# Graph attention on one core: the order of deep blocks in a batch's last two tiles, and who weighs them

## The chip, the core and the metric

The kernel runs on one core of a Trainium2 chip. The time is the device time of one launch in microseconds; lower is better. A core has five engines that run their own instruction queues in order and meet through semaphores: PE (TensorE, matmuls; PEld is its weight load), DVE (VectorE), ACT (ScalarE), POOL (GpSimd, which also issues the indirect DMAs) and SP (SyncE, which issues plain DMAs). The time before is the median of three runs, 1906.49 us (1903.19 to 1907.76).

## The reference

The layer is graph attention with a residual and a normalisation, for 16 batches of 1024 nodes with 512 features, 8 heads of 64. The adjacency matrix is the same for all batches and very sparse: a few nodes have many neighbours, most have a handful.

```python
def _L0_gnn_ref(x, adj, Wq, bq, Wk, bk, Wv, bv, Wo, bo):
    q = (x @ Wq + bq).reshape(b, n, H, HD)
    k = (x @ Wk + bk).reshape(b, n, H, HD)
    v = (x @ Wv + bv).reshape(b, n, H, HD)
    scores = jnp.einsum('bqhd,bkhd->bhqk', q, k) / jnp.sqrt(jnp.float32(HD))
    scores = scores + (1.0 - adj)[None, None, :, :] * -1000000000.0
    attn = jax.nn.softmax(scores, axis=-1)
    out = jnp.einsum('bhqk,bkhd->bqhd', attn, v).reshape(b, n, d)
    return out @ Wo + bo
x = _layernorm(x + _L0_gnn_ref(...), axis=-1)
```

## The kernel before

**Sparse work in tiles and blocks.** The nodes are ranked by their number of neighbours, and each batch is cut into 8 tiles of 128 nodes in that order. For each query the kernel gathers only the key and value rows that it has an edge to. The unit of this is a *block*: 128 gathered rows of keys and values (`kvg`, 128 x 1024 f32, 512 KB). In an *own* block `i` of a tile, row p holds the i-th neighbour of the tile's query p; `OWN` says how many own blocks each tile has. Nodes with more neighbours than that put the rest into *deep* blocks, in which 128 left-over edges of any queries of the tile stand side by side; `BLOCKS` says how many.

```python
OWN = (2, 1, 2, 3, 4, 5, 5, 7)
BLOCKS = (0, 0, 0, 0, 0, 0, 1, 5)
```

So tile 6 has 5 own blocks and 1 deep one, tile 7 has 7 and 5. Tile 1 (one key) takes no blocks: its value row `V1` is gathered alone and transposed with `turn` when block (7, 4) of its batch is reached. Tile 0 is worked on in batches 0 and 1 and in every odd batch, there for two batches at once. In all there are 530 blocks: 34 in batches 0, 1 and the odd ones, 32 in the even ones from 2 on. Of them 105 are first own blocks (i = 0), 329 further own blocks, and 96 deep ones.

**What a block costs.** `gather` issues the indirect DMA of the block's key and value rows on POOL (L1230), and for a deep block one of its query rows `qg` too (L1184), for an own block with i = 0 a plain load of the tile's query rows `qt` on SP (L1217). `products` multiplies query and key rows on DVE (L1251), `scores` sums them for each head on DVE (L1255), `exponentials` takes the exponential on ACT (L1266). `weigh` multiplies the value rows with the eight heads' weights: on ACT as eight activations of 128x64 (L1276), or on DVE as one instruction of 128x512 (L1280); `by_act` decides. An own block's weighed rows are then added to the tile's first ones on DVE (`add_own`, L1292). A deep block's rows are added by PE instead, which multiplies them with a 0/1 matrix `sums` that says to which query each row belongs (`add_up`, L1301 and L1302, four matmul instructions in all), into one PSUM buffer with the tag "sum". `normalise` divides a tile's rows by their sums on DVE when the next tile's first block comes, and for tiles 6 and 7 adds the PSUM buffer to the own sum first (L1313, L1314).

**The order.** All of it is written out by hand: a step n of the main loop (from L1470 on) emits the exponentials of block n+3, the products of n+4, the gathers up to n+8, the weighing of n+1 if DVE does it, the adding of n, the scores of n+4, the weighing of n+2 if ACT does it, and the deep sum of n. Each engine runs its own instructions in this order. The list `blocks` sets what block n is; before, a tile's own blocks come first and its deep blocks after them:

```python
blocks = [(b, t, i) for b in range(B) for t in tiles_of(b) if t != ONE_KEY for i in range(OWN[t] + BLOCKS[t])]
```

Between these steps PE works on the *fronts* of batches to come (transposes of x and the products for queries, keys and values, `pq`, `x`, `pp`, `z`) and on the output products `po` of tiles that are done. How many of these units a step gets is a credit: a share for the batch, weighted by `paced` with `load_of`, which counts the DVE work of a step. The results leave PSUM on DVE (q, w, g, kv) and on ACT, a step later. `KG_BUFS` = 8 buffers hold the gathered rows; a buffer is free again when its block has been weighed. Five buffers with the tag "qt" hold `qg` and `V1`.

**Who weighs.** `by_act` gives ACT all own blocks with i > 0; of all other blocks (first own and deep) it gives ACT those with an even n, and the first 17 of the program, except in the last batch, where DVE weighs them. In batches 1 to 14 this gives ACT 5 of 7 first blocks in odd batches and 4 of 6 in even ones, and 2 of 6 deep blocks in both.

Of the kernel before, what the change touches and what calls it, by code (L numbers as in the profile page):

```python
# [26 lines left out]
OWN = (2, 1, 2, 3, 4, 5, 5, 7)  # L27
BLOCKS = (0, 0, 0, 0, 0, 0, 1, 5)
# [6 lines left out]
LONE, ONE_KEY, ONE_KEY_AT, ONE_KEY_LAST = 64, 1, (7, 4), (3, 0)  # L35
# [142 lines left out]
def kernel(  # L178
# [37 lines left out]
    B, N, D = x.shape  # L216
# [13 lines left out]
    own = [SHORT_KEYS * t for t in SHORT]  # L230
# [3 lines left out]
    NBT = NB - OWN[ONE_KEY]  # L234
# [19 lines left out]
    with ExitStack() as main:  # L254
# [82 lines left out]
        def merged(b):  # L337
            return b >= PAIRED_FROM and b % 2 == 1

        def tiles_of(b):  # L340
            return [t for t in range(NT) if t or b < PAIRED_FROM or merged(b)]
# [828 lines left out]


        KG, QG, PV, PSUM, QT, RDEN, V1 = {}, {}, {}, {}, {}, {}, {}
        blocks = [(b, t, i) for b in range(B) for t in tiles_of(b) if t != ONE_KEY for i in range(OWN[t] + BLOCKS[t])]
        start = [min(n for n, block in enumerate(blocks) if block[0] == b) for b in range(B)] + [len(blocks)]

        def load_more():
# [90 lines left out]

        def by_act(n):
            b, t, i = blocks[n]
            return 0 < i < OWN[t] or n < total - NBT and (n % 2 == 0 or n < NBT // 2)  # L1270

        def weigh(n):
            v, pv = KG.pop(n), PV[n]
            if by_act(n):
                for h in range(HEADS):
                    nc.scalar.activation(  # L1276
                        pv[:, ts(h, HD)], v[:, ds(D + h * HD, HD)], AF.Copy, scale=pv[:, D + h:D + h + 1]
                    )
                return
            nc.vector.tensor_tensor(  # L1280
                pv[:, 0:D].rearrange("p (h d) -> p h d", d=HD),
                v[:, D:].rearrange("p (h d) -> p h d", d=HD),
                pv[:, D:, None].to_broadcast([P, HEADS, HD]), op=OP.mult,
            )
# [134 lines left out]
        total = len(blocks)  # L1419
# [4 lines left out]
        def load_of(n):  # L1424

            b, t, i = blocks[n]
            had = 2.0 + (not by_act(min(n + 1, total - 1))) + (0 < i < OWN[t])
            if i == 0:
                had += 3.0 if BLOCKS[blocks[n - 1][1]] else 1.3
            return had  # L1430
# [17 lines left out]
        with tc.manual_schedule():  # L1448
# [20 lines left out]
            n = -LEAD_IN  # L1469
            while n < total or plan or rest or urgent or done or finishing or spilled or lone_tiles or not guarded:  # L1470
# [6 lines left out]
                elif n in start:  # L1477

                    b = start.index(n)
                    left = sum(u[0] for u in fronts)  # L1480
# [11 lines left out]
                if 0 <= n + 1 < total and not by_act(n + 1):  # L1492
                    weigh(n + 1)
# [96 lines left out]
```

## Time and profile before

| | |
|---|---|
| median of the runs | 1906.49 us |
| the profiled execution | 1892.33 us, of which the span of the trace is 1890.4 us |
| mean granted PE clock | 0.989 |
| HBM traffic | 298 GB/s over the span |
| DVE scores, L1255 | 530 x 680 ns |
| DVE adding of own blocks, L1292 | 329 x 693 ns |
| gathers of key and value rows on POOL | 530, median 1017 ns each in the kv_pair ones, 6.4 us from issue to landing |

The profile shows one execution. An engine's busy time counts the time in which at least one of its instructions ran; the mean of one instruction is larger than busy time divided by number, because instructions overlap at their ends. Eight activations of one weighing on ACT take 8 x 864.6/3432 = 2.015 us. "Idle before" is the time for which an engine stood still ahead of an instruction, with what ended it. The prologue, in which the adjacency matrix is read and ranked, ends at about 136 us; after it a batch takes 100 to 134 us, and the last 26 us finish the output.

### The profile page before, as it was taken

How to read it: one execution, taken by the hardware profiler on the slowest of the kernel's cores; microseconds unless marked ns; L12 is line 12 of the kernel's file. 1: busy time of each engine (PE TensorE's matmuls, PEld its weight loads, DVE VectorE, ACT ScalarE, POOL GpSimd, SP SyncE). 2: the span in 40 equal slices, each digit the busy share in tenths (PEclk: the TensorE clock that was granted, in tenths of full speed). 3: DMA queues.
4: the chain of work that ended last, by engine and by line, in shares of the span. 5: the costliest groups of instructions: out<-in, count | busy, mean ns of one | idle time of the engine just before them, and what ended most of it. 6: DMA issues, size and time to landing. Idle time of an engine off the chain costs nothing. (4 is left out here: it accounts for less than half of the span.)

```text
span 1890.4 us, 25101 instructions
## 1 busy us (share of the span) xinstructions
PE 1815.1 (96%) x5149; PEld 878.2 (46%) x5149; DVE 1700.6 (90%) x3484; ACT 1531.7 (81%) x6016; POOL 1267.4 (67%) x1189
## 2 busy tenths in 40 slices
PE   7989999999999999999999999999999999999995
PEld 3434444444545454444445444444445444444442
DVE  6888889999999999899899989899999999997874
ACT  3627869979888988979798978989898989886794
POOL 1367766777677676757677676767666777656774
PEclk9989999999999999999999999999999999999997
DMA  7357787988889898888889898999889899989993
GB/s 280 114 168 226 233 307 227 315 295 294 308 287 316 305 328 283 305 288 307 312 292 335 271 334 274 314 304 310 301 307 326 293 356 310 314 277 340 334 319 117
DMA packets 188149, 544.63 MB, mean 288 GB/s; under 512 B 32602, under 2 KB 32622, under 8 KB 187986
## 3 DMA queue, kind: packets, MB, share of 16 engines
q0 software_dynamic: 116400, 382.82, 60.6%
q1 hardware_dynamic: 68510, 154.30, 21.8%
q10 hardware_dynamic: 3076, 5.82, 0.9%
q14 instruction: 120, 0.98, 0.2%
q8 instruction: 43, 0.70, 0.1%
HBM read 419.52 MB, written 144.34 MB: 298 GB/s over the span
## 5 line engine op out<-in xcount | busy, mean ns | idle before, releaser
L1276 ACT ACTIVATE pv<-kvg,pv 128x64 f32<-128x64 f32 x3432 | 864.6, 340 | 0.0
L1230 POOL DMA_INDIRECT kvg<-kv_pair,place_row x462 | 526.7, 1140 | 258.0 <-ACT pv L1276 73.3
L790 PE MATMUL po<-wo,oT 128*128 128x512 f32 x816 | 380.1, 596 | 1.0 <-ACT oT L1340 0.9
L790 PE MATMUL pq<-wq,xT 128*128 128x512 f32 x792 | 368.9, 597 | 0.4 <-DVE g L966 0.4
L1255 DVE TENSOR_REDUCE s<-qk 128x8 f32<-128x512 f32 x530 | 360.2, 680 | 7.5
L1251 DVE TENSOR_TENSOR qk<-qt,kvg 128x512 f32<-128x512 f32 x434 | 296.4, 683 | 22.2 <-DMA kvg<-kv_pair,place_row 22.1
L947 PE MATMUL pp<-t,s 128*128 128x512 f32 x504 | 237.4, 593 | 2.7 <-ACT sq_k L800 1.7
L947 PE MATMUL x<-b,xT 128*128 128x512 f32 x504 | 237.8, 594 | 0.8 <-ACT e L960 0.8
L790 PEld LDWEIGHTS po<-wo,oT 128*128 128x128 f32 x816 | 152.6, 191 | 166.8 <-issue 153.9
L1292 DVE TENSOR_TENSOR pv<-pv,pv 128x520 f32<-128x520 f32 x329 | 228.0, 693 | 0.7 <-ACT pv L1276 0.6
L790 PEld LDWEIGHTS pq<-wq,xT 128*128 128x128 f32 x792 | 149.2, 192 | 166.4 <-issue 155.0
L1266 ACT ACTIVATE pv<-s,absent 128x8 f32<-128x8 f32 x434 | 126.3, 293 | 79.8 <-DVE s L1255 76.2
L1001 POOL DMA_INDIRECT x<-in_x_dram,asked_row x120 | 130.2, 1085 | 88.3 <-PE pxT L748 40.5
L1125 POOL DMA_INDIRECT out_dram<-y,asked_row x129 | 144.8, 1122 | 35.7 <-issue 19.8
L800 ACT ACTIVATE sq_k<-kv 128x128 bf16<-128x128 f32 x512 | 150.9, 301 | 6.0 <-DVE kv L970 6.0
L947 PEld LDWEIGHTS pp<-t,s 128*128 128x128 f32 x504 | 94.2, 190 | 114.1 <-issue 101.4
L947 PEld LDWEIGHTS x<-b,xT 128*128 128x128 f32 x504 | 94.3, 191 | 111.5 <-issue 106.5
L1184 POOL DMA_INDIRECT qg<-q_rows,query_row x96 | 106.9, 1114 | 36.5 <-issue 24.7
L947 PE MATMUL z<-b,s 128*128 128x512 f32 x252 | 119.1, 595 | 6.5 <-DVE kv L975 6.5
L1029 POOL DMA_INDIRECT y<-in_x_dram,asked_row x93 | 104.5, 1124 | 27.5 <-issue 25.8
L947 PE MATMUL z<-t,s 128*128 128x512 f32 x252 | 120.0, 599 | 0.0
L947 PE MATMUL pp<-t,xT 128*128 128x512 f32 x252 | 118.4, 592 | 0.0
(276 smaller groups left out, 2766.7 us busy)
## 6 DMA issues: line engine op xcount, KB each, us to landing
kv_pair<-kv SPq DMA_DIRECT2D x98, 512.0 KB
q_rows<-q SPq DMA_DIRECT2D x106, 256.0 KB
qt<-q_rows SPq DMA_DIRECT2D x98, 256.0 KB
residual<-x SPq DMA_DIRECT2D x36, 256.0 KB
y<-residual SPq DMA_DIRECT2D x36, 256.0 KB
kv_rows<-kv SPq DMA_DIRECT2D x15, 512.0 KB
kvg<-kv_pair,place_row POOLq DMA_INDIRECT x462, 6.5
kv_pair<-kv SPq DMA_DIRECT2D x28, 256.0 KB
```

The lines of the kernel that those rows point to most:

```text
L790: nc.tensor.matmul(p, lhs(c), w[:, c, :], start=(c == 0), stop=(c == NPAIR - 1))
L800: nc.scalar.activation(sq, s[:, ts(h, P)], AF.Square, scale=scale, accum_out=sums[:, h:h + 1])
L947: nc.tensor.matmul(R[bank], l[:, ts(c, P)], right[:, c, :], start=(first and c == 0), stop=(c == 1), skip_group_check=True,)
L1001: nc.gpsimd.indirect_dma_start(out=y, out_offset=None, in_=x_rows, in_offset=bass.IndirectOffsetOnAxis(ap=asked_row[:, t:t + 1], axis=0), ...
L1125: nc.gpsimd.indirect_dma_start(out=out_rows[b, t], out_offset=bass.IndirectOffsetOnAxis(ap=rows, axis=0), in_=y, in_offset=None, element_o ...
L1184: nc.gpsimd.indirect_dma_start(out=q, out_offset=None, in_=q_rows[b % ROWS], in_offset=bass.IndirectOffsetOnAxis(ap=rows, axis=0))
L1230: nc.gpsimd.indirect_dma_start(out=KG[n], out_offset=None, in_=rows, in_offset=bass.IndirectOffsetOnAxis(ap=(place_row if b else key_row)[ ...
L1251: nc.vector.tensor_tensor(QK[n], q, KG[n][:, 0:D], op=OP.mult)
L1255: nc.vector.tensor_reduce(S[n], QK.pop(n).rearrange("p (h d) -> p h d", d=HD), axis=AX.X, op=OP.add)
L1266: nc.scalar.activation(PV[n][:, D:], S.pop(n), AF.Exp, bias=bias)
L1276: nc.scalar.activation(pv[:, ts(h, HD)], v[:, ds(D + h * HD, HD)], AF.Copy, scale=pv[:, D + h:D + h + 1])
L1292: nc.vector.tensor_tensor(PV[b, t], PV[b, t], pv, op=OP.add)
```

## The change

Two things change. The new function `blocks_of` gives the order of a tile's blocks: as before in batch 0 and in tiles without deep blocks, and otherwise with the deep blocks spread among the own ones. For tile 6 the order becomes 0, 1, 2, 5, 3, 4 (5 is the deep one), for tile 7 it becomes 0, 1, 7, 2, 8, 3, 9, 4, 10, 5, 11, 6 (7 to 11 are deep). And `by_act` no longer goes by the parity of n: ACT weighs own blocks with i > 0 and never a first block; of the deep blocks it weighs the ones of the program's first 17 blocks (there are none), those with an even n in batch 0, those with b + i even in batches 1 to 14, and none in the last batch.

```diff
-        blocks = [(b, t, i) for b in range(B) for t in tiles_of(b) if t != ONE_KEY for i in range(OWN[t] + BLOCKS[t])]
+
+        def blocks_of(b, t):
+
+            own, deep = list(range(OWN[t])), list(range(OWN[t], OWN[t] + BLOCKS[t]))
+            if b == 0 or not deep:
+                return own + deep
+            spread = max(1, len(own) // (len(deep) + 1))
+            left = len(own) - spread * len(deep)
+            for j, i in enumerate(deep):
+                own.insert(left + j * (spread + 1), i)
+            return own
+
+        blocks = [(b, t, i) for b in range(B) for t in tiles_of(b) if t != ONE_KEY for i in blocks_of(b, t)]
...
         def by_act(n):
             b, t, i = blocks[n]
-            return 0 < i < OWN[t] or n < total - NBT and (n % 2 == 0 or n < NBT // 2)
+            if i < OWN[t]:
+                return i > 0
+            return n < NBT // 2 or (n % 2 == 0 if b == 0 else b < B - 1 and (b + i) % 2 == 0)
```

## The prediction

> **What bounds the kernel now.** I read the totals first, then the chain that ended last, then a table of windows, one for each batch, then who waited for whom, and last the timeline of one batch boundary.
>
> ```profile
> PE 1815.1 (96%) x5149; PEld 878.2 (46%) x5149; DVE 1700.6 (90%) x3484; ACT 1531.7 (81%) x6016; POOL 1267.4 (67%) x1189
> ```
> TensorE (PE) is busy 96%, VectorE (DVE) 90%, ScalarE (ACT) 81%. Busy PE time can hide stretched matmuls, so the chain gives the pace:
>
> ```profile
> 1308.26 3.43 PE pq L790 x8
> ```
> 3.43 us / 8 = 0.429 us for a 512-column matmul instruction, wherever the chain runs through PE; most of the program's matmuls start at that distance. So PE is near its floor. What is left to win is what PE loses in stalls. The windows of nine batches (5 to 13), with the columns window, length, PE, PEld, DVE, ACT, POOL, clock, DMA share, GB/s:
>
> ```profile
> 697.00:806.00 109.00, 105.08 (x305) 51.15 (x303) 99.74 (x195) 92.22 (x376) 75.89 (x69) 1.00 0.87 303
> ...
> 909.00:1011.00 102.00, 100.80 (x294) 49.32 (x295) 99.08 (x196) 92.05 (x378) 74.00 (x68) 1.00 0.89 307
> ...
> sum 934.00, PE 906.93 PEld 442.47 DVE 878.63 ACT 810.96 POOL 649.81; mean PE 100.77 PEld 49.16 DVE 97.63 ACT 90.11 POOL 72.20
> ```
> A batch takes 934.00/9 = 103.78 us; PE is idle 3.0 us of it, DVE 6.15 us. Two engines are nearly full; ACT has 13.7 us left. Who waits, from 270 to 1740 us (batches 1 to 14), in us, times, longest:
>
> ```profile
> DVE qk L1251 <- DMA kvg<-kv_pair,place_row: 25.6, 13, 4.9
> DVE kv L975 <- PE z L947: 11.4, 11, 1.9
> ...
> PE sum L1301 <- DVE pv L1280: 11.0, 4, 3.7
> PE z L947 <- DVE kv L975: 6.1, 5, 2.4
> PE pm L858 <- DVE vsum L854: 5.6, 4, 1.9
> ...
> ACT pv L1266 <- DVE s L1255: 73.1, 66, 6.3
> ```
> PE's largest wait is for a deep block's weighed row, four times, 11.0 us. ACT waits for DVE, not DVE for ACT: making ACT shorter is worth nothing by itself. The largest of the four, at the end of batch 5:
>
> ```profile
> 788.74 1.17 POOL L1184 DMA_INDIRECT qg<-q_rows,query_row  x1 [0.30 <-issue]
> ...
> 796.55 1.01 POOL L1230 DMA_INDIRECT kvg<-kv_pair,place_row  x1 [0.30 <-ACT pv L1276]
> ...
> 804.94 0.69 DVE L1251 TENSOR_TENSOR qk<-qt,kvg 128x512 f32<-128x512 f32 x1 [4.28 <-DMA kvg<-kv_pair,place_row]
> ...
> 806.29 1.22 PE L1301 MATMUL sum<-pv,sums 128*128 128x256 f32 x2 [3.75 <-DVE pv L1280]
> ```
> DVE sat 4.28 us for the gathered rows of batch 6's first block. Their gather was issued at 796.55, 8.4 us before; from 771 us GpSimd (POOL) had no gap longer than the 0.30 us between two issues, because five deep blocks in a row asked for ten gathers (776.00 to 791.2), with stores and x loads behind them. PE then waited 3.75 us, and its clock fell:
>
> ```profile
> 798.65:810.00 11.35, 7.60 (x20) 4.22 (x19) 6.96 (x12) 4.17 (x18) 7.28 (x8) 0.85 1.00 385
> ```
> DMA was full (1.00) there, DVE busy 61%, the clock 0.85. "TensorE: Matmul & The Clock Gate" in the Trainium skill (HAM oscillation) says that PE idle for more than about 3.4 us is throttled; the 0.85 after 3.75 us agrees, and nothing in the sum uses the page.
>
> **The change, part by part.** (1) *Order.* From batch 1 on, tile 6 runs as own 0,1,2, deep, own 3,4 and tile 7 as own 0,1, then deep and own by turns. No instruction is added or removed: 96 deep blocks keep their products, scores, two gathers and two pairs of matmuls. The ten gathers of tile 7's deep blocks were issued in 15.2 us (776.00 to 791.2); they now come one pair for every two steps. At about 3.2 us a step (tile 7 took 762.5 to 799.4, twelve steps, 3.1 us each) that is 10 x 1.3 us of POOL in some 30 us, and the next batch's first gathers no longer stand behind a queue. SP's queue sees none of it: a tile's query rows are loaded with its own block 0, which stays first. What goes: PE's 11.0 us for deep rows, and the clock's loss after them, estimated from the window above as 0.15 x 7.60 = 1.1 us for the one long stall, some 2 us for all four. Bounds: nothing, if other transfers keep the gathers late (DMA share is 0.87 and 0.89 in the batch windows, so there is not much room); at best all the waits of PE listed above, 11.0 + 6.1 + 5.6 = 22.7, with the clock about 25. I take 13 for this: the mechanism is plain in the trace, and POOL's queue is the only thing at that place which the order makes.
>
> "Perfetto Trace Analysis" in the Trainium skill (Optimization Strategy) says that a kernel whose most contended engine changes over time may gain from interleaving these stretches. The trace has the stretches: 745 to 768 us is bound by ACT (22.37 of 23.00 us), 798.65 to 810 by DMA.
>
> (2) *Who weighs.* Before, ACT weighs 429 blocks (3432/8) and DVE 101. After the new rule ACT keeps all 329 own blocks with i > 0 and weighs 44 deep ones: 373; DVE 157. The 56 that move: seven first blocks in batch 0; in each of the seven odd batches 1 to 13 five first blocks go to DVE and two deep ones to ACT, +3, 21 in all; in each of the seven even batches 2 to 14 four first blocks, 28. The last batch changes nothing but its order.
>
> ```profile
> L1276 ACT ACTIVATE pv<-kvg,pv 128x64 f32<-128x64 f32 x3432 | 864.6, 340 | 0.0
> ...
> L1280 DVE TENSOR_TENSOR pv<-kvg,pv 128x512 f32<-128x512 f32 x101 | 68.9, 683 | 0.0
> ```
> ACT loses 56 x 864.6/429 = 56 x 2.015 = 113 us; DVE gains 56 x 0.683 = 38.2 us, of which 7 x 0.683 = 4.8 in batch 0, where 250 to 270 us shows DVE at 16.38 of 20.00 and PE at 20.00: hidden. The other 49 cost 33.5 us, 2.4 us a batch. Their cover is DVE's idle 6.15 us a batch. A batch's floor by DVE becomes 97.63 + 2.4 = 100.0 us, by PE it stays 100.8. So the cover holds on the mean, but it is thin: in the quietest window (909 to 1011) DVE idles 2.92 us, and an odd batch adds 2.05. What is late if it gives way: DVE runs its queue in order, so behind the extra weighing stand the sum of the own blocks, the next scores, then w, g and kv, for which PE waits. Bounds: 0 (all covered) to +33.5 (none). I take +4: about 0.3 us a batch, nearer to the covered end, since DVE's waits (25.6 for gathers, 11.4 for z) are what the order shortens.
>
> A rule against it: "SBUF — State Buffer" (Who interferes with whom) says that a DVE instruction with two SBUF inputs blocks a GpSimd instruction that reads SBUF. If every one of the 49 held up a gather for its length, POOL would be 33.5 us later in all. The trace has gathers of 1017 ns at the median beside a full DVE and 1000 ns in batch 0, where DVE had room, so I give it nothing.
>
> (3) *ACT's relief.* The 113 us are worth nothing where ACT waits for DVE. Where ACT is full (745 to 768 us) it frees the gather buffers late; POOL's gathers waited 88.0 us for ACT's weighing over the whole span. In even batches tiles 6 and 7 now give ACT 12 of 18 blocks, in odd ones 14 as before, without the run of twelve. PE's waits for kv and vsum in these tiles (6.1 + 5.6) might shrink by a third: I take -4, bounds 0 and -11.7 (the same waits as in the upper bound of (1), so not to be added to it).
>
> (4) *Pacing.* `load_of` counts a step's DVE work, so PE's units are dealt out anew within each batch; their number is the same. Of the deep sums, tile 7's first now comes at the tile's third block instead of its eighth, into the one "sum" buffer that tile 6's result has left two steps earlier: two steps are 6 us against 1.5 us for reading it, nothing.
>
> Sum: -13 + 4 - 4 = **-13 us** on the profiled execution, 1890.4 to 1877 us of span (1892.3 to 1879 with the 1.9 around it). That execution lies 14.2 us under the median of the runs, 1906.49; the difference is carried over: **1893.5 us**, -0.7%.
>
> **Rivals.** *DVE takes the bound* (slower). One mechanism: 2.4 us more of DVE work in each of batches 1 to 14, in an engine that idles 6.15 us, while the idle time that it has is waiting that returns in another place. It decides once DVE's busy share of a batch passes about 98%; the quiet batches stand at 97.1% (99.08/102.00) and would come to 99%. All of it on the path, with the 13 us won, is 33.5 - 13 = +20, 1927; half of it +4; with the stalls staying as well and half of it, +17. Centre 1917. For it: ACT waits 73.1 us for DVE, so work moves from the engine that waits to the one waited for. Against it: 25.6 us of DVE's idle time hang on gathers that the order brings forward.
>
> *No change.* The four stalls go, but gathers are late elsewhere, since POOL and DMA have the same work; or gain and price are equal (13 against 13). 1906.
>
> *More than forecast.* All three of PE's waits go and DVE's price is covered: -25, 1881.
>
> *A buffer that is held longer.* The one-key tile's row sits in the five "qt" slots from tile 7's start to its own block 4, which now comes three steps later. If slots went strictly in turn, the last deep query of each batch would wait for it. The trace excludes this: in batch 5 that row was gathered at 747.2 and read by PE from 793.3, yet the fifth query gather after it went out at 788.74. I give it 1 in 100.
>
> **How the numbers follow.** Forecast (1885 to 1901) 0.40; more than forecast (1868 to 1885) 0.13; no change (1901 to 1912) 0.18; DVE bound (1912 to 1930) 0.28; buffer 0.01. A measurement of this kernel tells about 0.3%, 5.7 us, from no change. Faster: 0.40 + 0.13, 0.53; within: 0.17; slower: 0.30. The range leaves out the end of the large gain and of the uncovered price: 1873 to 1921. The likeliest case alone is 1885 to 1901.
>
> **What would show it.** Right: PE's wait for deep rows under 3 us in batches 1 to 14; DVE's wait for kvg under half of 25.6; no window at a batch boundary with a clock of 0.85; a batch's window near 102.8 us with DVE busy about 100. DVE bound: batches of 104 us or more with DVE above 98% and PE's waits for kv, g or vsum longer than now. No change: as many stalls, named by other lines. Wrong outright: ACT's weighing not 373 x 8 = 2984 instructions.

## The result, and the profile after

The changed kernel takes 1933.35 us (median of six runs, 1927.07 to 1944.06), beside 1906.17 us (1902.95 to 1910.45) for the kernel before on the same chip. The ratio is 1.0146, with a 95% interval of 1.0114 to 1.0179: 27 us slower, where 13 us faster was forecast, and outside the range.

The totals of the changed kernel's page, for the profiled execution (span 1930.4 us, mean granted clock 0.981):

```profile
PE 1831.2 (95%) x5149; PEld 881.3 (46%) x5149; DVE 1736.2 (90%) x3540; ACT 1433.4 (74%) x5568; POOL 1286.2 (67%) x1189
...
L1290 ACT ACTIVATE pv<-kvg,pv 128x64 f32<-128x64 f32 x2984 | 752.0, 340 | 0.2 <-issue 0.2
```

The weighing went where the diff says: 2984 activations on ACT, 373 blocks, and 56 more instructions on DVE (3540 against 3484). ACT is 98.3 us shorter and DVE 35.6 us longer. PE does the same 5149 matmuls, and the time is longer. (Lines after the diff's first hunk moved: the gather is now L1242, the products L1263, the scores L1267, the exponential L1278, ACT's weighing L1290, DVE's L1294, the deep sum L1315 and L1316.)

The table of windows of the changed kernel, again one for each of batches 5 to 13 (columns: window, length, busy time of PE, PEld, DVE, ACT and POOL, clock, DMA share, GB/s):

```profile
825.00:927.00 102.00, 100.98 (x295) 49.38 (x294) 99.06 (x193) 83.80 (x336) 73.23 (x67) 1.00 0.89 305
927.00:1035.00 108.00, 104.05 (x299) 50.33 (x298) 101.26 (x198) 86.90 (x350) 73.71 (x68) 1.00 0.86 304
1035.00:1142.00 107.00, 97.31 (x277) 47.04 (x276) 97.90 (x191) 80.32 (x319) 73.17 (x67) 0.97 0.84 288
...
sum 950.00, PE 913.81 PEld 443.38 DVE 900.36 ACT 754.96 POOL 665.50; mean PE 101.53 PEld 49.26 DVE 100.04 ACT 83.88 POOL 73.94
```

A batch takes 950/9 = 105.56 us, 1.78 more than before. DVE's busy time rose by 2.41 us a batch, from 97.63 to 100.04, just as worked out in the prediction. But its idle time, which was to take this up, went only from 6.15 to 5.52 us. DVE's share is highest in the second of the nine windows (825 to 927 us), 99.06/102.00 = 97.1%, as in the fullest window before; the mean share is 94.8% (94.1% before). PE idles 4.0 us a batch instead of 3.0, and its busy time for the same matmuls rose by 0.76 us, from 100.77 to 101.53.

The waits of the changed kernel from 270 to 1740 us (us, times, longest):

```profile
ACT pv L1278 <- DVE s L1267: 111.8, 107, 4.9
...
PE z L947 <- DVE kv L975: 17.0, 7, 7.4
...
DVE qk L1263 <- DMA kvg<-kv_pair,place_row: 11.7, 10, 3.6
...
PE sum L1315 <- DVE pv L1294: 4.1, 2, 3.6
```

The order did what it says: DVE's wait for gathered rows fell from 25.6 to 11.7 us, PE's wait for deep rows from 11.0 to 4.1. In their place PE waits for `kv` (6.1 before, 17.0 now, one wait of 7.4), and ACT waits longer for DVE's scores (73.1 before, 111.8 now). The long wait lies in batch 8, at the start of tile 7, and the timeline there is:

```profile
1108.30 0.43 DVE L774 TENSOR_TENSOR s<-xT 128x256 f32<-128x256 f32 x1 [2.88 <-ACT pv L1290]
...
1110.46 0.69 DVE L1294 TENSOR_TENSOR pv<-kvg,pv 128x512 f32<-128x512 f32 x1
...
1112.27 0.68 DVE L1099 TENSOR_TENSOR y<-po,y 128x512 f32<-128x512 f32 x1
1112.39 0.30 ACT L1278 ACTIVATE pv<-s,absent 128x8 f32<-128x8 f32 x1 [4.62 <-DVE s L1267]
...
1115.01 0.68 DVE L1328 TENSOR_TENSOR o<-sum,pv 128x512 f32<-128x512 f32 x1
...
1116.58 0.68 DVE L975 TENSOR_TENSOR kv<-z,g 128x512 f32<-128x512 f32 x1
...
1117.32 1.22 PE L947 MATMUL z<-b,s 128*128 128x512 f32 x1 [7.41 <-DVE kv L975]
```

DVE stood idle for 2.88 us, and from 1108.30 to 1116.58 it never stops. It works off the tile change in its own order: four parts of `s`, products, a weighing, an adding, scores, the two output instructions of another tile, products and scores of a second block, and the normalising of tile 6. `kv` stands last in this row of 8.28 us, and PE waits for it. Then PE's clock falls; the windows of the changed kernel around it:

```profile
1110.00:1118.00 8.00, 0.68 (x1) 0.50 (x2) 7.90 (x18) 1.32 (x4) 5.36 (x5) 0.74 0.84 264
1118.00:1126.00 8.00, 8.00 (x20) 3.54 (x19) 4.46 (x8) 3.31 (x11) 1.76 (x2) 0.83 0.71 246
```

DVE is busy 7.90 of 8 us while PE does one matmul, and then DVE has only 4.46 us to do while PE, at a clock of 0.83, catches up. That is how it looks here, at the longest stall: DVE is idle, then full for some steps, then idle again, and the idle time ahead and behind does not help the steps between.

### The profile page after: what moved, and what is told of

It is laid out like the page before. It is cut to its first block, busy times and chain, and to the rows that moved or that the text cites. A ratio compares the mean times of both kernels' runs of the same rounds, so it can differ in the third digit from the quotient of the medians.

```text
span 1930.4 us, 24614 instructions
## 1 busy us (share of the span) xinstructions
PE 1831.2 (95%) x5149; PEld 881.3 (46%) x5149; DVE 1736.2 (90%) x3540; ACT 1433.4 (74%) x5568; POOL 1286.2 (67%) x1189
## 5 line engine op out<-in xcount | busy, mean ns | idle before, releaser
L1290 ACT ACTIVATE pv<-kvg,pv 128x64 f32<-128x64 f32 x2984 | 752.0, 340 | 0.2 <-issue 0.2
L1242 POOL DMA_INDIRECT kvg<-kv_pair,place_row x462 | 531.1, 1149 | 266.3 <-issue 87.0
L1267 DVE TENSOR_REDUCE s<-qk 128x8 f32<-128x512 f32 x530 | 360.7, 680 | 7.2 <-DVE qk L1263 0.4
L1263 DVE TENSOR_TENSOR qk<-qt,kvg 128x512 f32<-128x512 f32 x434 | 296.8, 684 | 11.3 <-DMA kvg<-kv_pair,place_row 7.4
L1278 ACT ACTIVATE pv<-s,absent 128x8 f32<-128x8 f32 x434 | 127.2, 295 | 137.4 <-DVE s L1267 108.0
L1001 POOL DMA_INDIRECT x<-in_x_dram,asked_row x120 | 136.0, 1133 | 91.8 <-PE pxT L748 36.1
L1125 POOL DMA_INDIRECT out_dram<-y,asked_row x129 | 149.3, 1157 | 36.9 <-issue 25.3
L947 PE MATMUL z<-b,s 128*128 128x512 f32 x252 | 124.8, 619 | 20.8 <-DVE kv L975 19.6
```

What stands on the lines that cost most here:

```text
L947: nc.tensor.matmul(R[bank], l[:, ts(c, P)], right[:, c, :], start=(first and c == 0), stop=(c == 1), skip_group_check=True,)
L1001: nc.gpsimd.indirect_dma_start(out=y, out_offset=None, in_=x_rows, in_offset=bass.IndirectOffsetOnAxis(ap=asked_row[:, t:t + 1], axis=0), ...
L1125: nc.gpsimd.indirect_dma_start(out=out_rows[b, t], out_offset=bass.IndirectOffsetOnAxis(ap=rows, axis=0), in_=y, in_offset=None, element_o ...
L1242: nc.gpsimd.indirect_dma_start(out=KG[n], out_offset=None, in_=rows, in_offset=bass.IndirectOffsetOnAxis(ap=(place_row if b else key_row)[ ...
L1263: nc.vector.tensor_tensor(QK[n], q, KG[n][:, 0:D], op=OP.mult)
L1267: nc.vector.tensor_reduce(S[n], QK.pop(n).rearrange("p (h d) -> p h d", d=HD), axis=AX.X, op=OP.add)
```

## The experiments

All times below come from five rounds against the kernel before on the same chip. The chips differ by 2%: the kernel before took 1929.16 us in the first set (e1 to e4), 1889.78 in the second (a1, e5 to e7), 1890.59 in the third (e8 to e11) and 1890.09 in the fourth (e12 to e14). So ratios are compared, not times; 1% is 18.9 us in the last three sets. Times named in the expectations of e1 to e4 are to be read against the 1906 us of the result.

**First set: the parts of the diff one by one.** e1 keeps the new order and gives each block to the engine that had it before:

```diff
+        was = {block: n for n, block in enumerate(sorted(blocks))}
         def by_act(n):
             b, t, i = blocks[n]
-            if i < OWN[t]:
-                return i > 0
-            return n < NBT // 2 or (n % 2 == 0 if b == 0 else b < B - 1 and (b + i) % 2 == 0)
+            k = was[b, t, i]
+            return 0 < i < OWN[t] or k < total - NBT and (k % 2 == 0 or k < NBT // 2)
```

> The new order of blocks, every block weighed by the same engine as before (ACT 429, DVE 101). If the owner rule is the cost (56 more weighings on DVE, 38 us, none of it covered), the order keeps its forecast gain: 1885 to 1900 us, and PE waits for deep rows under 5 us. If the order is the cost (PE's waits for kv in tiles 6 and 7 grew from 6 to 17 us), most of the 27 us are here: 1920 to 1935.

e2 is the kernel before with the new `by_act` alone, in the old order.

> The old order of blocks with the new owner rule (ACT 373, DVE 157). Owner theory: all of the loss and the four stalls at batch ends still there, 1930 to 1945 us. Order theory: close to before, 1902 to 1912.

e3 is the changed kernel with first blocks by the old rule, deep blocks by the new one (443 blocks on ACT, 87 on DVE):

```diff
         def by_act(n):
             b, t, i = blocks[n]
+            k = was[b, t, i]
             if i < OWN[t]:
-                return i > 0
+                return i > 0 or k < total - NBT and (k % 2 == 0 or k < NBT // 2)
```

> The changed kernel with the 70 first blocks of before back on ACT; deep blocks as in the change (ACT 443, DVE 87). Owner theory: faster than the changed kernel by 70 x 0.683 us or nearly so, 1885 to 1905. Order theory: 1920 to 1935, as the changed kernel.

e4 is the kernel before with the seven first blocks of batch 0 on DVE (`if b == 0 and i == 0: return False`), since batch 0 had grown by 8 us in the trace of after.

> The kernel before, with only batch 0's seven first blocks weighed by DVE. Batch 0 became 8 us longer in the changed kernel, though its order is the same. Owner theory: 5 to 9 us slower than before, 1911 to 1915. Rival: batch 0 grew for what runs beside it from batch 1 on, no change, 1904 to 1908.

| kernel | ratio | 95% interval |
|---|---|---|
| e1, order alone | 0.9970 | 0.9929 to 1.0011 |
| e2, owners alone | 1.0092 | 1.0044 to 1.0139 |
| e3, first blocks back on ACT | 0.9930 | 0.9889 to 0.9971 |
| e4, batch 0's first blocks on DVE | 1.0020 | 0.9973 to 1.0066 |

The owners cost and the order does not; and of the owners it is the first blocks. With them back, the kernel is faster than before. e2 came out between its two forecasts: the 1930 to 1945 us of the owner theory are 1.0125 to 1.0204 of 1906.17. e4 decides nothing: its interval holds both answers. Batch 0 turned out to differ between executions of the same program (142.1 us in the trace of after, 134.0 in that of a1 below, from its first score sum to that of batch 1), so its growth was not the change's doing.

**Second set: is it DVE's load, ACT's relief, or the place?** a1 is the changed kernel once more, as a yardstick on this chip.

> The changed kernel once more, beside the next three on one chip. Both theories: 1.012 to 1.018 of the kernel before.

e5 has e3's first blocks on ACT, and in batches 1 to 14 DVE weighs own block 2 of tiles 3 to 7 instead. So both engines have the numbers of the changed kernel (157 and 373), at other places:

```diff
+                if i == 2 and 0 < b < B - 1 and t > 2:
+                    return False
```

> First blocks weighed as before, and instead 70 own blocks (block 2 of tiles 3 to 7, batches 1 to 14) moved from ACT to DVE: DVE 157 and ACT 373, as in the changed kernel. If the load on DVE is the price, wherever it falls: as the changed kernel, 1.010 to 1.020 of before. If it is that first blocks meet the end of the tile before (normalise) on DVE: as with the firsts back, 0.990 to 1.000.

e6 is e3 with ACT keeping the 70 first blocks, and a DVE instruction of a weighing's size that changes no value (the max of a tile with itself) at the place of each, counted by the pacing like a weighing:

```diff
+        def extra(n):
+            return n < total and blocks[n][2] == 0 and by_act(n)
...
-            had = 2.0 + (not by_act(min(n + 1, total - 1))) + (0 < i < OWN[t])
+            had = 2.0 + (not by_act(min(n + 1, total - 1)) or extra(n + 1)) + (0 < i < OWN[t])
...
+                if 0 <= n + 1 and extra(n + 1):
+                    nc.vector.tensor_tensor(bq_bc, bq_bc, bq_bc, op=OP.max)
```

> First blocks weighed by ACT as before (ACT 443), and DVE given 70 instructions more of the same shape that change no value, at the places where the changed kernel weighs those blocks. If ACT's relief is worth nothing: as the changed kernel, 1.012 to 1.018. If the relief is worth something, slower than it by up to 20 us, 1.020 to 1.028. Below 1.005 the load is not the cause.

e7 goes further than e3: in the changed kernel ACT weighs all first blocks but those of the last batch (`return i > 0 or b < B - 1`), 471 blocks on ACT, 59 on DVE.

> New order, deep blocks as in the change, and all first blocks of batches 0 to 14 on ACT: ACT 471, DVE 59, 28 fewer on DVE than with the firsts back (ratio 0.993). If DVE's load has a price everywhere, 28 x 0.683 = 19 us off at about 0.86 on the path: 0.982 to 0.988. If ACT becomes the bound of tiles 2 and 3: 0.995 or more.

| kernel | DVE / ACT blocks | ratio | 95% interval |
|---|---|---|---|
| a1, changed kernel | 157 / 373 | 1.0136 | 1.0109 to 1.0162 |
| e5, weighed elsewhere | 157 / 373 | 1.0018 | 1.0000 to 1.0035 |
| e6, DVE's load without ACT's relief | 87 + 70 / 443 | 1.0135 | 1.0108 to 1.0162 |
| e7, all first blocks on ACT | 59 / 471 | 0.9930 | 0.9905 to 0.9956 |

e6 and a1 agree: what ACT was spared is worth nothing that can be told from noise (each interval is 5 us to either side), and what costs is 70 instructions more in DVE's queue at these places (and what the pacing makes of them). e5 and a1 have the same engine totals and lie 1.2% apart (22 us), so it is not DVE's total that decides. But e5 moves the pacing too, since `load_of` follows its owners, so the 22 us are not the place of the load alone. e7 fits neither of its forecasts (0.982 to 0.988, or 0.995 and more): taking 28 more first blocks off DVE earned nothing beyond e3 (0.9930 both, with the pacing that follows). The windows of batches 5 to 13 in e5:

```profile
sum 935.00, PE 910.18 PEld 443.59 DVE 900.90 ACT 746.34 POOL 650.45; mean PE 101.13 PEld 49.29 DVE 100.10 ACT 82.93 POOL 72.27
```

and in a1:

```profile
sum 945.00, PE 911.06 PEld 442.46 DVE 899.61 ACT 754.48 POOL 659.29; mean PE 101.23 PEld 49.16 DVE 99.96 ACT 83.83 POOL 73.25
```

DVE is equally busy, 100.1 and 100.0 us a batch; a batch takes 103.9 us in e5 and 105.0 in a1. In e5 DVE's idle time has shrunk to 3.8 us a batch, so more of it can be used than the changed kernel uses. It is not free: e5 lies 0.85% above the same kernel without the 70 (e10 below, 0.9933, on another chip), 16 us or a third of the 47.8 that they issue, pacing included. Nor is ACT's longer wait for DVE's scores the price: from 270 to 1740 us it is 142.9 us in e5, 120.3 in a1, and only 68.9 in e6, which is as slow as a1.

**Third set: the load, or the pacing by it?** `load_of` weighs a step with the weighing that DVE does in it, and the credit for PE's units goes by that weight. So each first block that moves to DVE also draws units to its step. e8 is the changed kernel, paced as if the first blocks were where e3 has them; e9 is e3, paced as if they were where the changed kernel has them. The owners themselves stay (shown for e8; in e9 `paced_as` holds the changed kernel's rule):

```diff
+        def paced_as(n):
+            b, t, i = blocks[n]
+            k = was[b, t, i]
+            if i < OWN[t]:
+                return i > 0 or k < total - NBT and (k % 2 == 0 or k < NBT // 2)
+            return n < NBT // 2 or (n % 2 == 0 if b == 0 else b < B - 1 and (b + i) % 2 == 0)
...
-            had = 2.0 + (not by_act(min(n + 1, total - 1))) + (0 < i < OWN[t])
+            had = 2.0 + (not paced_as(min(n + 1, total - 1))) + (0 < i < OWN[t])
```

> The changed kernel (first blocks on DVE), but PE's units dealt out over the steps as in the kernel with the firsts back: only the weights of the pacing differ. Load theory (DVE's extra work at the first blocks is the price): 1.010 to 1.020 of before. Pacing theory (the units dealt out anew make PE and DVE miss each other): 0.990 to 1.002.

> The reverse: first blocks back on ACT, PE's units dealt out as in the changed kernel. Load theory: as with the firsts back, 0.988 to 1.000. Pacing theory: 1.008 to 1.018.

e10 is e3 again, on this chip. e11 is the kernel before, old order, with all first blocks but the last batch's on ACT (`return i < OWN[t] and (i > 0 or b < B - 1) or ...`).

> The changed kernel with the 70 first blocks back on ACT once more, beside the others on one chip: 0.990 to 0.997.

> The kernel before, in its own order, with all first blocks of batches 0 to 14 on ACT (28 fewer on DVE). If DVE's load is the price everywhere: 0.988 to 0.995. If the four stalls at the batch ends, which the old order keeps, are what is left to win: 0.997 to 1.005.

| ratio (95% interval) | paced as e3 | paced as the changed kernel |
|---|---|---|
| first blocks as in e3 | e10: 0.9933 (0.9908 to 0.9958) | e9: 1.0036 (1.0017 to 1.0054) |
| first blocks as in the change | e8: 1.0055 (1.0039 to 1.0071) | a1: 1.0136 (1.0109 to 1.0162) |

Both cost by themselves. The load costs 1.22% or 1.00% (23 and 19 us, 21 on the mean), which is 44% of the 70 x 0.683 = 47.8 us that it issues. The pacing costs 1.03% or 0.81% (19 and 15 us, 17 on the mean), without one instruction more. Together 2.03%, 38 us. (a1 ran on another chip than the other three; its ratio is taken over.) e8 and e9 each came out between their two forecasts, because neither theory alone was right. Of the 22 us between a1 and e5, 15 are thus what a1 pays for its weights (a1 less e8); e8 is only 0.37% (7 us, on two chips) above e5. e11 comes to 0.9969 (0.9952 to 0.9986), at the edge of its second forecast: taking 28 first blocks off DVE helps in the old order too, by 6 us of the 19 that they issue, with the pacing that follows.

What the pacing does can be seen in batch 8's wait. e10, first blocks on ACT and its own pacing:

```profile
1084.91 3.78 PE L947 MATMUL z<-b,s 128*128 128x512 f32 x4 [3.86 <-DVE kv L975]
```

and e9, which differs from it in the pacing alone:

```profile
1099.11 3.78 PE L947 MATMUL z<-b,s 128*128 128x512 f32 x4 [7.16 <-DVE kv L975]
```

The wait before the same matmuls is 7.16 us instead of 3.86. DVE's queue shows where the 3.3 us come from. In e10 `kv` stands right behind the output instructions (L1099 and L1100) and ahead of tile 6's normalising (`o`):

```profile
1082.82 0.68 DVE L1099 TENSOR_TENSOR y<-po,y 128x512 f32<-128x512 f32 x1
...
1084.18 0.68 DVE L975 TENSOR_TENSOR kv<-z,g 128x512 f32<-128x512 f32 x1
...
1086.23 0.68 DVE L1330 TENSOR_TENSOR o<-sum,pv 128x512 f32<-128x512 f32 x1
```

In e9 it has slipped behind the products and scores of a further block and the normalising, as in the changed kernel's timeline above:

```profile
1094.07 0.68 DVE L1099 TENSOR_TENSOR y<-po,y 128x512 f32<-128x512 f32 x1
...
1096.80 0.68 DVE L1336 TENSOR_TENSOR o<-sum,pv 128x512 f32<-128x512 f32 x1
...
1098.38 0.68 DVE L975 TENSOR_TENSOR kv<-z,g 128x512 f32<-128x512 f32 x1
```

So it comes 4.31 us after the output's first instruction instead of 1.36. The wait is 7.4 in a1 and in e6 (same weights as e9), and 4.4 in e8 (e10's weights, the changed kernel's load):

```profile
1096.03 2.98 PE L947 MATMUL z<-b,s 128*128 128x512 f32 x4 [4.44 <-DVE kv L975]
```

So the longest stall of the changed kernel is lengthened by the dealing out of units far more than by the weighing that stands in it (3.3 us against 0.6). The deep sums show the same: PE waits for DVE's deep rows (270 to 1740 us) 1.3 us in e8 and 1.4 in e10, but 5.4 in a1, 6.7 in e9 and 3.4 in e6. Part of the price is the clock: over the runs the mean granted clock is 0.990 in e10 and 0.988 in e8, but 0.986 in e9 and 0.984 in a1.

**Fourth set: order and pacing apart from each other.** e12 is e1 again on a quieter chip. e13 is the kernel before (old order, old owners) with the changed kernel's owners in `load_of` alone. e14 is e7 with e3's owners in `load_of`, so that the pacing counts 28 weighings that DVE no longer does.

> The new order, every block weighed by the same engine as before, once more (first time 0.997, interval 0.993 to 1.001, on a noisier chip). If the order alone earns the forecast 13 us: 0.990 to 0.995. If the gain of the kernel with the firsts back (0.993) came from its 14 deep blocks fewer on DVE: 0.997 to 1.002.

> The kernel before, all instructions on the same engines, but PE's units dealt out as if DVE weighed what it weighs in the changed kernel. If the pacing's price (0.8 to 1.0% in the new order) belongs to the weights: 1.006 to 1.012. If it needs the new order: 0.998 to 1.004.

> New order, all first blocks of batches 0 to 14 on ACT, PE's units dealt out as in the kernel with the firsts back. If weights of the pacing that count first blocks cost whatever the load: 0.985 to 0.991 would need none of them, so 0.991 to 0.997 here. If a pacing that does not fit the load is what costs: 0.998 to 1.006.

e12 comes to 0.9997 (0.9981 to 1.0014): the order alone, with the pacing that follows from it, is worth nothing that can be measured. e13 comes to 1.0069 (1.0047 to 1.0092): the weights cost 13 us in the old order as well, with every instruction on the engine that it had before. Its waits from 270 to 1740 us:

```profile
ACT pv L1266 <- DVE s L1255: 94.3, 71, 7.1
DVE qk L1251 <- DMA kvg<-kv_pair,place_row: 31.6, 23, 4.6
PE sum L1307 <- DVE pv L1286: 16.6, 9, 4.2
...
PE z L947 <- DVE kv L975: 7.0, 7, 1.4
```

Each of these is longer than in the kernel before (73.1, 25.6, 11.0 and 6.1 us): with the same work dealt out otherwise, engines wait longer for each other. e14 comes to 0.9967 (0.9952 to 0.9982), against 0.9930 for e7: 0.4% given back, again by weights alone, though runs on two chips are compared. The waits of e12 from 270 to 1740 us:

```profile
PE z L947 <- DVE kv L975: 14.9, 6, 4.9
DVE qk L1264 <- DMA kvg<-kv_pair,place_row: 14.0, 14, 2.4
...
PE sum L1315 <- DVE pv L1294: 1.4, 1, 1.4
```

With the order alone, the four long waits for deep rows are gone (11.0 to 1.4 us; 6.8 in e1, on the noisier chip), and DVE's for gathers are shorter (25.6 to 14.0). PE's wait for `kv` took most of it back (6.1 to 14.9). PE's saving and its loss nearly cancel: -9.6 and +8.8, and its whole idle time in this stretch is 32.5 us before and 32.3 in e12.

With that idle time of PE, from 270 to 1740 us in one trace of each, the ratios go in nearly the same order: 21.4 us in e7, 24.4 in e10, 28.4 in e11, 29.3 in e14, 32.3 in e12, 33.5 in e5, 36.9 in e8, 38.9 in e9, 39.6 in e13, 42.6 in e6 and 44.2 in a1. DVE's busy time over the whole program does not order them: it is 1733.2 us in e5, 1734.4 in e8, 1735.1 in a1 and 1736.1 in e6.

"Perfetto Trace Analysis" in the Trainium skill (Optimization Strategy) says that interleaving stretches with different bounds may help. Here, by e12, doing so changed nothing by itself.

**What beats both.** e10 (0.9933) and e7 (0.9930) are both faster than the kernel before, by 12 to 13 us, and cannot be told apart. The windows of batches 5 to 13 in e10:

```profile
sum 925.00, PE 904.61 PEld 441.55 DVE 875.93 ACT 823.72 POOL 643.84; mean PE 100.51 PEld 49.06 DVE 97.33 ACT 91.52 POOL 71.54
```

A batch takes 102.8 us, with DVE at 97.3 and ACT at 91.5: about what the prediction had drawn for the change itself, reached with the first blocks on ACT. The waits of e7 from 270 to 1740 us:

```profile
ACT pv L1278 <- DVE s L1267: 19.4, 23, 3.9
DVE qk L1263 <- DMA kvg<-kv_pair,place_row: 15.2, 12, 5.4
...
PE z L947 <- DVE kv L975: 10.3, 7, 2.3
```

Here ACT hardly waits for DVE any more (19.4 us, 73.1 before), and PE's longest wait for `kv` is 2.3 us.

## Why the prediction was wrong, point by point

**The sum that the runs give.** In per cent of the kernel before, over the last three sets: order -0.03 (e12); the new rule for deep blocks, with the pacing that follows from it, -0.64 (e10 less e12; it leaves DVE 14 deep blocks fewer, and in odd batches all six change hands); 70 first blocks on DVE +1.1 and the pacing by them +0.9 (means of the square above). That is +1.36 in all, a1's ratio; the steps lead from the kernel before to a1, so their sum is no further test. In us: -0.6 - 12.1 + 21.0 + 17.4 = +25.7. Each term is good to some 6 us.

The forecast was -13, some 39 us less. Of these, 17 lie in (4), the pacing, which the prediction put at nothing; 12 in (1), the order; 5 in (2), who weighs (+9 net, not +4); and 4 in (3). So the step that failed most is (4), and next to it (1).

**(1) Order, -13: not earned.** The first half of the mechanism was right and its signs came: gathers earlier, deep rows in time. What failed is the tacit step that a wait removed is time removed. PE's saved waits returned as waits for `kv`: in e12 one of 3.9 us (batch 8) and one of 3.5 (batch 9) at the change from tile 6 to tile 7, and one of 4.9 near the end of batch 13. Why they came is not shown; the order also changes the weights of `load_of` step by step, and no run holds these fixed. The lower bound that the prediction gave, nothing, was the result, though for another reason than the one named there (other transfers).

**(2) Who weighs, +4: +9 net, and the cover failed.** The count was right to the instruction and DVE's busy time to 0.04 us a batch (100.0 forecast, 100.04 measured). The cover was wrong. "So the cover holds on the mean" takes an idle time of 6.15 us a batch as room that any work can use. But it gave only 0.63 us a batch (6.15 to 5.52) to the 2.41 us that were added. A first block is weighed at a tile's change, where normalising and the next scores queue up as well, as the timeline of batch 8 shows. The 70 first blocks cost 21 us before the pacing, and the new rule for deep blocks gave 12 back, with its pacing. The net of +9 comes near the forecast's +4 by this cancelling, which the prediction did not have: it netted the blocks to 56 equal instructions. That the place counts is shown for load and pacing together (e5, 22 us less); for the load alone e8 less e5 leaves 7 us, with e5's own pacing in it.

**(3) ACT's relief, -4: nothing.** e6 equals a1. The prediction's own first reading, that making ACT shorter is worth nothing where ACT waits for DVE, should have ruled here.

**(4) Pacing, nothing: +17 us, the largest miss.** The prediction noted that PE's units are dealt out anew, and costed only the PSUM buffer. The second term of the measured sum in size was an edit nobody wrote: `load_of` calls `by_act`, so a change of owner shifts units. e13 shows a price of the weights with no other change at all, 13 us.

**The rivals.** *DVE takes the bound* had the sign, the engine and half of the price on the path (44% measured), but the pacing lay outside it, so its top, 1927, is under 1933.35. Its condition was wrong: DVE's share passed 98% in none of the nine batches (97.1% at most), and the price was paid at 94.8% on the mean. *No change* by late gathers is excluded by DVE's shorter waits for them. *A buffer that is held longer*: from 270 to 1740 us no query gather of the changed kernel shows a wait longer than 0.3 us, the time between two issues.

**What was named as a sign.** ACT's 2984 instructions: as said. DVE's wait for gathers under half: yes, 11.7. PE's wait for deep rows under 3 us: no, 4.1 in after, though 1.4 with the order alone. No clock of 0.85 at a batch's boundary: yes, but the clock falls to 0.74 and 0.83 at the boundary of tiles 6 and 7 in batch 8 instead. A batch of 102.8 us with DVE at 100: DVE yes, the batch 105.6. Of the signs of *DVE bound*, batches of 104 us or more and longer waits of PE for `kv` came, and DVE above 98% did not.

**What stays open.** Which units, drawn to which steps, make DVE and PE miss each other was not taken apart beyond the one stall of batch 8; the argument that the weights send units to the very steps that DVE is fullest in fits the code (a first block's weighing is emitted one step before its tile begins, and the weight of the tile's first step, with the normalising, follows), but no run moved the weight of a single step. Nor was it tried whether weights fitted to the new order make it worth more than e7 has.

## What to carry to other kernels

An engine's mean idle time is not room for any work: here 44% of the added work came out as time although DVE idled 6 us a batch. Before costing added work at nothing, look at the steps that it falls into, and at what is queued behind it there. Follow every caller of a function that you change: here a rule of ownership was also the planner's input, and that cost nearly as much as the work moved. A wait that goes is a gain only if the next engine in line was ready, so ask of the trace what the waiting engine would have waited for next.

## What the runs showed of the hardware

The kernel before took 1906.17, 1929.16, 1889.78, 1890.59 and 1890.09 us by median in the five sets of runs, 2% apart, more than any single term of the sum above. Batch 0 took 134.0 and 142.1 us in two executions of one program. And a stall of 7.41 us cost PE more than its length: the granted clock was 0.74 in the window of the stall and still 0.83 over the 8 us after it, which is, as an estimate, another 0.17 x 8 = 1.4 us.
